# First stage of a two-layer attention kernel: the shared v products of two blocks in four 64x64 quarters, and a new order of the stage

## The chip, the cores and the metric

The kernel runs on one core of a Trainium2 chip. Its time is the device time of one execution in microseconds; the times of a kernel are given as the median of several runs. TensorE (PE) multiplies, VectorE (DVE), ScalarE (ACT) and GpSimd (POOL) do elementwise work, SyncE (SP) issues most DMA transfers.

## The reference

Two layers work on x of shape (4, 192, 128, 128), all in f32. Only the first part of the first layer matters here:

```python
qkv = dwconv3x3(conv1x1(x, w_qkv), w_dw)      # 192 -> 768 channels, then a 3x3 convolution of each channel alone
q, k, v, l = jnp.split(qkv, 4, axis=1)
...                                            # q, k normalised over the pixels, attention between channels
out = jnp.einsum('bhcd,bhdn->bhcn', attn, v)
pooled = jnp.mean(l, axis=(2, 3), keepdims=True)
...
```

The second layer is a dilated attention on the first one's output; its code isn't touched.

## The kernel before

The first stage (`project`, `plan_projection`) makes q, k and v by a 1x1 convolution, convolves v over 3x3, and writes q and k unconvolved to DRAM (the second stage convolves them). It works in 64 blocks: two images at a time, four image rows, 512 pixels of each image. The 192 input channels are 128 and 64. A block's `xt` tile (128 partitions, 3 x 512) holds the 128 first channels of both images in columns 0 and 1, and in column 2 the last 64 channels of the one image on partitions 0 to 63 and those of the other on 64 to 127 (`loads`, L347 to L351).

Each output tile of 128 channels is a sum of two products in one PSUM bank: a full one over 128 input channels (`first_half` L357, `first_half_v` L490) and one over the last 64 (`second_half` L362, `second_half_v` L495). The second ones use half of the array's rows, and those of the two images run side by side. There are three such tiles of q and k and one of v for each image. The 64 channels of v that are left make one tile of both images together, `shared_tile`: first (j = 0, L367) a full product with `wv2`, a 128x128 weight with the 64x64 weight twice on its diagonal and zeros elsewhere; then (j = 1, L371) two products of 128 rows by 64 columns, one for each image, side by side.

ScalarE moves the finished banks on: q and k to `us` (L375) and from there to DRAM (`qk_store`, L379), v to a ring of 12 rows (`v_evict`, L386), which is three blocks long. Three spare rows behind the ring's end are copied once per round (L175). The 3x3 convolution of a block's v (`plan_conv`) needs its neighbours' rows. For the 128-channel tiles ScalarE writes the centre tap to `pa` in PSUM (L397, one buffer), and VectorE adds eight taps (`tap`, L404), the last into `v_False`. For the shared tile ScalarE makes scaled copies (`side`, L416) and GpSimd adds them up (`side_sum`, L427). VectorE also adds up each block's x (`totals`, L441) for l's mean, and GpSimd keeps its edge columns (L445).

No loop sets the order. Every piece is given to a `Schedule` with an engine, a rank, a cost and what it comes after. The planner simulates the engines with these costs: an engine that is free takes the ready piece with the smallest rank, where on PE a piece of another array shape than the last counts `change_rank` more, and a change of shape takes `change` more time (0.13 and 0.05 in this stage before). The order found is emitted for each engine and is fixed from then on; the engines wait for one another by semaphores. `hold` makes the piece that takes a buffer come after the last user of the buffer that is taken again; the buffers of a pool are given out in the order of the first users' ranks. The products share six PSUM banks (`pu`), and `xt` has four buffers.

Of the kernel before, what the change touches and what calls it, by code (L numbers as in the profile page):

```python
# [13 lines left out]
B, C, H, W = 4, 192, 128, 128  # L14
# [9 lines left out]
PX = RB * W  # L24
RING = 12
# [11 lines left out]
class Schedule:  # L37
# [10 lines left out]
    def add(self, engine, rank, cost, run, after=(), shape=None, latency=LATENCY):  # L48
        op = dict(engine=engine, rank=rank, cost=cost, run=run, shape=shape, latency=latency, seq=len(self.ops))
        op.update(after=list(after), first=[], users=[], issued=[])  # L50
        self.ops.append(op)
        return op

    def hold(self, pool, bufs, first, last):

        self.pools.setdefault((pool, bufs), []).append((first, last))
# [131 lines left out]
    return t.rearrange("p (r w) -> p r w", w=W)  # L188


FULL, COLS, ROWS, QUADS = "128x128", "128x64", "64x128", "128x32"
HALVES = [slice(0, G), slice(G, 128)]
EXTRA = 2 * B * CH0 + B
SM = EXTRA + B * 2 * CH0
# [4 lines left out]
AROUND = (0, 1, 2, 6, 7, 8, 3, 5)  # L199

PLACES = {
# [111 lines left out]
def project(tc, x, load, other_loads, sums, qk_dram, v_dram, v2_dram):  # L316

    nc = tc.nc  # L320
    with ExitStack() as ctx:
        wts = ctx.enter_context(tc.tile_pool(name="p1w", bufs=1))
        wx, wx2, wv2, dwv = (load(wts, n) for n in ("wx", "wx2", "wv2", "dwv"))
        stage = Stage(ctx, tc, "p1", dict(xt=4, us=6, v=3, v2=3, side=3, ring=1), dict(pu=6, pa=1))
        rings = stage.pools["ring"]
        vboth = rings.tile([128, RING + SPARE, 2, W + 2], F32, tag="vboth", name="vboth")
        ring = [vboth[:, :, 0], vboth[:, :, 1]]
        ring.append(rings.tile([128, RING + SPARE, W + 2], F32, tag="ring2", name="ring2"))
        for r in ring:
            nc.gpsimd.memset(r[:, :, 0 : W + 2 : W + 1], 0.0)  # L330
        plan_projection(nc, stage, x, wx, wx2, wv2, dwv, vboth, ring, sums, qk_dram, v_dram, v2_dram)
        for i, run in enumerate(other_loads):
            stage.schedule.add("SP", 8 + i, 0.5, run)
        stage.run(tc)


def plan_projection(nc, stage, x, wx, wx2, wv2, dwv, vboth, ring, sums, qk_dram, v_dram, v2_dram):
    add, hold, tile_of, tiles = stage.schedule.add, stage.hold, stage.tile, stage.tiles
    mm = nc.tensor.matmul
    flat = lambda a: a.rearrange("c h w -> c (h w)")  # L340

    def place(n):
        p, i = divmod(n, NB)
        return 2 * p, slice(i * RB, (i + 1) * RB)

    def loads(n):
        im0, rows = place(n)  # L347
        t = tile_of("xt", ("xt", n), (128, 3, PX))
        nc.sync.dma_start(t[:, 0:2, :], x[im0 : im0 + 2, 0:128, rows, :].rearrange("b c h w -> c b (h w)"))
        for im in range(2):  # L350
            nc.sync.dma_start(t[HALVES[im], 2, :], flat(x[im0 + im, 128:C, rows, :]))  # L351

    def first_half(n, mt):

        for im in range(2):
            pu = tile_of("pu", ("pu", n, mt, im))
            mm(pu, wx[:, mt * 128 : (mt + 1) * 128], tiles["xt", n][:, im, :], start=True, stop=False)  # L357
# [3 lines left out]
            w = wx2[HALVES[im], mt * 128 : (mt + 1) * 128]  # L361
            mm(tiles["pu", n, mt, im], w, tiles["xt", n][HALVES[im], 2, :], start=False, stop=True)  # L362

    def shared_tile(n, j):

        if j == 0:
            mm(tile_of("pu", ("pu", n, 3, 2)), wv2, tiles["xt", n][:, 2, :], start=True, stop=False)  # L367
            return
        for im in range(2):
            to = tiles["pu", n, 3, 2][HALVES[im]]  # L370
            mm(to, wx[:, 2 * C + 128 :], tiles["xt", n][:, im, :], start=False, stop=True)  # L371
# [78 lines left out]
    def edge_row(n, to, of):  # L450
        nc.vector.tensor_reduce(sums[n // NB][2][:, :, to : to + 1], tiles["xt", n][:, :, of : of + W], AX.X, ALU.add)

    def plan_products(n):
        load_op = add("SP", n - 1.5, 0.5, (loads, n), latency=6.0)
        users = []
        shared = add("PE", n + 0.52, 0.86, (shared_tile, n, 0), [load_op], FULL)
        users.append(shared)
        for mt in range(4):
            t = n + 0.5 * (mt // 2) + 0.01 * (mt % 2)
            first, second = (first_half_v, second_half_v) if mt == 3 else (first_half, second_half)  # L460
            args = (n,) if mt == 3 else (n, mt)
            a = add("PE", t, 1.72, (first, *args), [load_op], FULL)
            b = add("PE", t + 0.2, 0.86, (second, *args), [a], ROWS)
            users += [a, b]
            if mt == 3:
                continue
            evs = [add("ACT", t + 0.25, 0.56, (qk_evict, n, mt, im), [b]) for im in range(2)]
            for ev in evs:
                hold("pu", a, ev)
            hold("us", evs[0], add("SP", t + 0.3, 0.3, (qk_store, n, mt), evs, latency=5.0))  # L470
            evs[1]["first"].append(evs[0])
        last = add("PE", n + 0.75, 0.9, (shared_tile, n, 1), [shared], COLS)
        users.append(last)
        for m in range(3):
            ev = add("ACT", n + 0.8, 0.56, (v_evict, n, m), [last if m == 2 else b])
            stage.fill("u", m, n, RING, ev)
            stage.repeat(ring, "u", m, n, RING, n + 0.83)
            hold("pu", shared if m == 2 else a, ev)
        users.append(add("DVE", n + 0.5, 1.7, (totals, n), [load_op]))
        users += [add("POOL", n + 0.3 * k, 0.2, (edges, n, k), [load_op]) for k in range(3)]  # L480
        if n % NB == 0:
            users.append(add("DVE", n, 0.5, (edge_row, n, 2, 0), [load_op]))
        if n % NB == NB - 1:
            users.append(add("DVE", n, 0.5, (edge_row, n, 0, PX - W), [load_op]))
        hold("xt", load_op, *users)

    def first_half_v(n):
# [7 lines left out]
            mm(tiles["pu", n, 3, im], w, tiles["xt", n][HALVES[im], 2, :], start=False, stop=True)  # L495

    def plan_conv(n):
        prev = first = add("ACT", n + 2, 1.2, (centre, n, False), latency=0.3)
        for j, t in enumerate(AROUND):
            prev = add("DVE", n + 2 + (j + 0.9) / 8, 1.22, (tap, n, t, j == 7), [prev])  # L500
            for m in range(2):
                stage.read("u", m, n, t // 3 - 1, prev)
        for m in range(2):
            stage.read("u", m, n, 0, first)
        hold("pa", first, prev)
        store = add("SP", n + 3.0, 0.3, (v_store, n, False), [prev], latency=5.0)
        hold("v", prev, store)
        prev = first = add("ACT", n + 2, 0.7, (centre, n, True))
        stage.read("u", 2, n, 0, first)
        for j, t in enumerate(AROUND):  # L510
            sd = add("ACT", n + 2 + (j + 0.4) / 8, 0.68, (side, n, t))
            stage.read("u", 2, n, t // 3 - 1, sd)
            prev = add("POOL", n + 2 + (j + 0.9) / 8, 1.26, (side_sum, n, t), [sd, prev])
            hold("side", sd, prev)
        store = add("SP", n + 3.0, 0.3, (v_store, n, True), [prev], latency=5.0)
        hold("v2", first, store)

    for n in range(2 * NB + 1):
        if n < 2 * NB:
            plan_products(n)  # L520
        if n >= 1:
            plan_conv(n - 1)
# [826 lines left out]
def _laid_out(inputs):  # L1349
    import numpy as np  # L1350

    a = {k: np.asarray(v) for k, v in inputs.items()}
# [12 lines left out]
    def both(w):  # L1365
        n = w.shape[1] // G
        z = np.zeros((2, G, n, 2, G), w.dtype)
        for im in range(2):
            z[im, :, :, im] = w.reshape(G, n, G)
        return z.reshape(128, n, 128)  # L1370
# [15 lines left out]
    for dy in range(3):  # L1386
# [5 lines left out]
    wx = wq[: 3 * C].T  # L1392
# [4 lines left out]
        "wx2": rest(wx),  # L1397
        "bands": bands,
        "cuttaps": cuttaps.reshape(4 * CH0, 2 * HEADS0, 3, 2 * CH0),
        "wv2": both(wx[128:, 2 * C + 128 :])[:, 0],  # L1400
        "wl": wq[3 * C :].T[:128],
        "wl2": rest(wq[3 * C :].T),
        "dwl": halves(dw[3 * C :]),
# [44 lines left out]
```

## Time and profile before

| | us |
|---|---|
| median of three runs (4406.96 to 4409.0) | 4407.45 |
| the profiled execution | 4406.01 |
| its span, first to last instruction | 4404.2 |
| first stage on PE | 8.27 to 852.7 |
| last tap of the first stage on DVE ends | 878.6 |

Over the whole span PE is busy 97%, DVE 86%, POOL 75%, ACT 59%. PE carries 80% of the chain that ended last; the first stage's groups on it are, with their busy time over the whole run:

| line | what | instructions | busy us |
|---|---|---|---|
| L357 | full products, q and k | 768 | 366.0 |
| L362 | products over the last 64 channels, q and k | 744 (to 830 us) | 193.3 |
| L490 | full products, v | 248 (to 830 us) | 119.3 |
| L371 | shared tile, 128x64 | 248 (to 830 us) | 66.9 |
| L495 | products over the last 64 channels, v | 248 (to 830 us) | 66.1 |
| L367 | shared tile, 128x128 with wv2 | 124 (to 830 us) | 63.3 |

A product of f32 shows as two instructions in the trace. A matmul's length in the trace is that of its way through the array; the distance of two starts is what it costs in a row. Times of one engine's groups overlap a little at their edges.

### The profile page before, as it was taken

The numbers are of one execution on the slowest core, as the hardware profiler recorded it, in microseconds if no ns is written. First come the engines' busy times: TensorE is split into PE (matmuls) and PEld (weight loads), VectorE is DVE, ScalarE is ACT, GpSimd is POOL, SyncE is SP. The second block draws the span as 40 slices with busy tenths as digits, with TensorE's granted clock in tenths as the row PEclk, the third lists the DMA queues.
The fourth block names the chain that finished last, engine by engine and source line by source line (L and its number), as shares of the span: only waits on it lengthen the run. The fifth ranks groups of instructions, "written<-read, shape, count | busy, mean of one in ns | idle before, by whom it ended". The sixth has DMA issues, their size and how long they took to land.

```text
span 4404.2 us, 64532 instructions
## 1 busy us (share of the span) xinstructions
PE 4289.9 (97%) x20608; PEld 1649.0 (37%) x20608; DVE 3806.3 (86%) x5492; ACT 2593.1 (59%) x4858; POOL 3319.0 (75%) x3407
## 2 busy tenths in 40 slices
PE   9999999899999998999999999999999999999996
PEld 3333333354445642333333333333333333333321
DVE  7998889855555546999999999999999999999996
ACT  7888888833333337656656556556566566566531
POOL 6777778811111112999999999999999999999998
PEclk9999999999999999999999999999999999999997
DMA  8777787668887648666566666656565665665521
GB/s 268 245 243 237 230 258 251 198 154 175 178 174 172 143 109 177 131 133 135 126 130 132 126 130 129 136 123 128 127 136 124 131 134 125 133 131 125 116 53 32
DMA packets 502386, 675.81 MB, mean 153 GB/s; under 512 B 138576, under 2 KB 320412, under 8 KB 502048
## 3 DMA queue, kind: packets, MB, share of 16 engines
q1 hardware_dynamic: 464160, 504.94, 43.2%
q0 software_dynamic: 37888, 166.74, 20.9%
q8 instruction: 166, 2.72, 0.3%
q14 instruction: 172, 1.41, 0.1%
HBM read 277.72 MB, written 201.33 MB: 109 GB/s over the span
## 4 chain that ended last, share of the span: by engine, by line
PE 80%; DVE 13%; issue 3%; POOL 2%; DMA 1%; ACT 1%; SPq 0%; DVEq 0%; POOLq 0%; ACTq 0%
PE pc L640 12%; PE sc L1105 9%; PE ex L1227 8%; PE pu L357 8%; PE ph L872 7%; PE pkv L1026 5%; DVE term L1233 4%; PE pu L362 4%; PE gram L712 4%; PE pkv L1029 4%; PE q L1086 4%; PE q L1083 4%; DVE prod L1094 3%; PE pu L490 2%; PE po L1249 2%
## 5 line engine op out<-in xcount | busy, mean ns | idle before, releaser
L1236 POOL TENSOR_TENSOR acc<-acc,term 128x512 f32<-128x512 f32 x1536 | 2034.6, 1330 | 133.0 <-DVE term L1233 45.5
L1233 DVE TENSOR_TENSOR term<-ex,vring 128x512 f32<-128x512 f32 (+2 forms) x1596 | 1000.1, 663 | 55.3 <-PE ex L1227 43.1
L1094 DVE TENSOR_TENSOR prod<-q,kring 128x1536 f32<-128x1536 f32 (+1 forms) x600 | 1007.3, 1688 | 16.8 <-PE q L1083 7.3
L427 POOL TENSOR_TENSOR v_True<-v_True,side 128x512 f32<-128x512 f32 (+1 forms) x512 | 647.9, 1267 | 169.7 <-ACT side L416 141.9
L404 DVE SCALAR_TENSOR_TENSOR pa<-vboth,dwv,pa 128x1024 f32<-128x1024 f32 (+1 forms) x448 | 574.3, 1282 | 76.9 <-ACT pa L397 54.4
L1227 PE MATMUL ex<-e_sb,spread 108*128 108x512 bf16 x1728 | 567.2, 387 | 37.5 <-DVE term L1233 31.2
L627 POOL COPY band<-band 64x384 f32<-64x384 f32 x192 | 95.8, 499 | 563.9 <-DMA band<-in_bands 506.5
L640 PE MATMUL pc<-u,band 64*64 64x508 f32 (+1 forms) x4608 | 518.3, 593 | 1.4 <-ACT ring L386 1.4
L1039 ACT COPY kring<-pkv 64x512 f32<-64x512 f32 x384 | 223.3, 581 | 419.5 <-PE pkv L1029 413.9
L924 DVE SCALAR_TENSOR_TENSOR pa<-hboth,posw,pa 128x1024 f32<-128x1024 f32 (+1 forms) x320 | 408.3, 1276 | 38.8 <-ACT pa L912 19.7
L1105 PE MATMUL sc<-prod,pick 128*32 128x512 f32 x3456 | 428.9, 598 | 1.8 <-DVE prod L1094 1.8
L653 DVE BATCH_NORM_STATS2 stats<-pc 128x6 f32<-128x128 f32 x1440 | 303.0, 283 | 141.1 <-ACT conv L649 141.0
L649 ACT COPY conv<-pc 128x512 f32<-128x512 f32 x384 | 210.6, 587 | 296.9 <-PE pc L640 288.7
L1026 PE MATMUL pkv<-y,wkv 128*128 128x512 f32 x768 | 365.5, 598 | 11.8 <-DMA y<-moved 8.7
L1227 PEld LDWEIGHTS <-spread 108*128 108x128 bf16 x1728 | 133.4, 98 | 647.0 <-issue 626.7
L872 PE MATMUL ph<-xv,mix 128*64 128x512 f32 (+1 forms) x1024 | 374.3, 596 | 0.5 <-DMA mix<-mixed 0.5
L357 PE MATMUL pu<-xt,wx 128*128 128x512 f32 x768 | 366.0, 613 | 8.3 <-DMA xt<-in_x 8.3
L1252 ACT COPY o<-po 128x512 f32<-128x512 f32 x192 | 106.2, 588 | 433.5 <-PE po L1249 227.9
L416 ACT ACTIVATE side<-ring,dwv 128x512 f32<-128x512 f32 (+1 forms) x512 | 350.8, 736 | 13.9 <-POOL v_True L427 13.1
L956 ACT ACTIVATE side<-hring,posw 128x512 f32<-128x512 f32 (+1 forms) x512 | 340.9, 710 | 9.6 <-DMA side<-side 7.7
L640 PEld LDWEIGHTS pc<-u,band 64*64 64x64 f32 x4608 | 189.5, 134 | 301.2 <-issue 284.7
L1039 ACT COPY vring<-pkv 64x512 f32<-64x512 f32 x384 | 223.9, 583 | 45.9 <-PE pkv L1029 32.6
(165 smaller groups left out, 6073.8 us busy)
## 6 DMA issues: line engine op xcount, KB each, us to landing
qk_dram<-us SPq DMA_DIRECT2D x192, 512.0 KB
u<-qk_dram SPq DMA_DIRECT2D x384, 256.0 KB
side<-side POOLq DMA_DIRECT2D x124, 768.0 KB, 7.1
xt<-in_x SPq DMA_DIRECT2D x64, 512.0 KB
v_dram<-v_False SPq DMA_DIRECT2D x64, 512.0 KB
xv<-in_x SPq DMA_DIRECT2D x128, 256.0 KB
xv<-v_dram SPq DMA_DIRECT2D x128, 256.0 KB
y<-moved POOLq DMA_DIRECT2D x64, 512.0 KB, 5.2
```

The costliest lines, as they stand in the source:

```text
L357: mm(pu, wx[:, mt * 128 : (mt + 1) * 128], tiles["xt", n][:, im, :], start=True, stop=False)
L404: nc.vector.scalar_tensor_tensor(by_row(to[:, o : o + length]), by_row(vboth[:, at : at + length, :, t % 3 : t % 3 + W]), dwv[:, 0, t : t ...
L427: nc.gpsimd.tensor_add(v[:, rows, :], v[:, rows, :], z[:, rows, :])
L640: nc.tensor.matmul(pcs[e][r * G : (r + 1) * G, :, to], band[at, e, c, dx, :], u[at, e, c, :].rearrange("p (b w) -> p b w", w=W)[:, :, of], ...
L872: mm(to, w[:, cols], tiles["xv", n, j, im], start=j == 0, stop=j == 2)
L1026: mm(rows3(tile_of("pc", key)), w, tiles["y", n, im], start=True, stop=False)
L1039: nc.scalar.copy(rows[HALVES[im], :, pad : pad + W], rows3(tiles["pkv", n, pair, im])[HALVES[e]])
L1094: nc.vector.tensor_mul(to[:, :, px].rearrange("p t (r w) -> p t r w", w=W), q.unsqueeze(1).to_broadcast([128, 3, *q.shape[1:]]), three,)
L1105: mm(sc[quad * 32 : (quad + 1) * 32, :], pick[:, QR - 4 * row : QR - 4 * row + 32], tiles["prod", n, k // NT, k % NT // 3][:, k % 3, :], s ...
L1227: mm(rows3(tile_of("ex", ("ex", n, g, t))), spread[:, t, :], e_sb, start=True, stop=True)
L1233: nc.vector.tensor_mul(rows3(to[:, px]), rows3(ex[:, px]), win)
L1236: nc.gpsimd.tensor_add(tiles["acc", n, g], tiles["acc", n, g], tiles.pop(("term", n, g, t)))
```

## The change

Three edits, all in the first stage.

The full product with `wv2` is gone, and so is `wv2`. For a pair of blocks n and n + 1, `shared_pair` makes the same sums by four products of 64 rows by 64 columns: for block n image 0 from array rows 0 to 63 to columns 0 to 63 and image 1 from rows 64 to 127 to columns 64 to 127; for block n + 1 the other two quarters. Since in these the rows and the columns are crossed, the images of the odd block must be exchanged: `loads` fetches the last 64 channels of odd blocks a second time, images swapped, to a new pool `xs` of two buffers. `shared_tile` keeps only its 128x64 products.

All ranks of the stage's pieces come from a table, `PLACES1`, by name and, for most, by the block's parity. The planner's costs for some pieces are changed, `change` is 0.2 and `change_rank` 3.9276.

```diff
+    "shared_pair": (-10.5337, 0),
+    "first_half0_0": (-11.0801, 0),
+    "first_half1_0": (-10.6217, 0),
+    "first_half2_0": (-10.7952, 0),
+    "first_half_v_0": (-10.8873, 0),
+    "first_half0_1": (-11.1547, 0),
+    "first_half1_1": (-11.0694, 0),
+    "first_half2_1": (-10.6251, 0),
+    "first_half_v_1": (-10.5823, 0),
+    "totals": (-11.7036, 0),
+    "centre0": (-10.4919, 0),
+    "tap": (-12.1176, 0),
...
-        stage = Stage(ctx, tc, "p1", dict(xt=4, us=6, v=3, v2=3, side=3, ring=1), dict(pu=6, pa=1))
+        stage = Stage(ctx, tc, "p1", dict(xt=4, xs=2, us=6, v=3, v2=3, side=3, ring=1), dict(pu=6, pa=1), change=(0.2, 3.9276))
...
+        if n % 2:
+            other = tile_of("xs", ("xs", n))
+            for im in range(2):
+                nc.sync.dma_start(other[HALVES[1 - im]], flat(x[im0 + im, 128:C, rows, :]))
...
-    def shared_tile(n, j):
-
-        if j == 0:
-            mm(tile_of("pu", ("pu", n, 3, 2)), wv2, tiles["xt", n][:, 2, :], start=True, stop=False)
-            return
+    def shared_pair(n):
+
+
+        for e in range(2):
+            to = tile_of("pu", ("pu", n + e, 3, 2))
+            of = tiles["xs", n + 1] if e else tiles["xt", n][:, 2, :]
+            for im in range(2):
+                half = HALVES[(im + e) % 2]
+                mm(to[HALVES[im]], wx2[half, 2 * C + 128 :], of[half], start=True, stop=False)
+
+    def shared_tile(n):
+
         for im in range(2):
             to = tiles["pu", n, 3, 2][HALVES[im]]
             mm(to, wx[:, 2 * C + 128 :], tiles["xt", n][:, im, :], start=False, stop=True)
...
+    def at(name, n, k=0):
+        first, step = PLACES1.get(name) or PLACES1[f"{name}_{n % 2}"]
+        return n + first + step * k
+
+    load_ops, pairs = {}, {}
+
     def plan_products(n):
-        load_op = add("SP", n - 1.5, 0.5, (loads, n), latency=6.0)
-        users = []
-        shared = add("PE", n + 0.52, 0.86, (shared_tile, n, 0), [load_op], FULL)
-        users.append(shared)
+        if n % 2 == 0:
+            for m in (n, n + 1):
+                load_ops[m] = add("SP", at("loads", m), 0.5, (loads, m), latency=6.0)
+            two = [load_ops[n], load_ops[n + 1]]
+            pairs[n] = pairs[n + 1] = add("PE", at("shared_pair", n), 0.86, (shared_pair, n), two, QUARTERS)
+        load_op, shared = load_ops[n], pairs[n]
+        users = [shared]
+        if n % 2:
+            hold("xs", load_op, shared)
...
-        last = add("PE", n + 0.75, 0.9, (shared_tile, n, 1), [shared], COLS)
+        last = add("PE", at("shared1", n), 0.86, (shared_tile, n), [shared], COLS)
...
-            prev = add("DVE", n + 2 + (j + 0.9) / 8, 1.22, (tap, n, t, j == 7), [prev])
+            prev = add("DVE", at("tap", n, j), 1.24, (tap, n, t, j == 7), [prev])
```

More of the change, by code (lines that the diff above doesn't have):

```diff
@@ L188, in rows3 @@
     return t.rearrange("p (r w) -> p r w", w=W)
-FULL, COLS, ROWS, QUADS = "128x128", "128x64", "64x128", "128x32"
+FULL, COLS, ROWS, QUADS, QUARTERS = "128x128", "128x64", "64x128", "128x32", "64x64"
 HALVES = [slice(0, G), slice(G, 128)]
@@ L199 @@
 AROUND = (0, 1, 2, 6, 7, 8, 3, 5)
+PLACES1 = {
+    "loads": (-10.5941, 0),
+    "shared_pair": (-10.5337, 0),
+    "first_half0_0": (-11.0801, 0),
+    "second_half0_0": (-9.1745, 0),
+    "qkev0_0": (-12.2520, 0),
+    "qkst0_0": (-12.2622, 0),
+    "first_half1_0": (-10.6217, 0),
+    "second_half1_0": (-11.4242, 0),
+    "qkev1_0": (-12.1789, 0),
+    "qkst1_0": (-5.5430, 0),
+    "first_half2_0": (-10.7952, 0),
+    "second_half2_0": (-8.3455, 0),
+    "qkev2_0": (-12.1932, 0),
+    "qkst2_0": (-19.1101, 0),
+    "first_half_v_0": (-10.8873, 0),
+    "second_half_v_0": (-6.7221, 0),
+    "shared1_0": (-11.0929, 0),
+    "vev0_0": (-9.4687, 0),
+    "vev1_0": (-11.4742, 0),
+    "vev2_0": (-11.4466, 0),
+    "totals": (-11.7036, 0),
+    "edges": (-10.7962, 0.00202),
+    "edge_row": (-16.1943, 0),
+    "first_half0_1": (-11.1547, 0),
+    "second_half0_1": (-12.4945, 0),
+    "qkev0_1": (-11.6485, 0),
+    "qkst0_1": (-2.8082, 0),
+    "first_half1_1": (-11.0694, 0),
+    "second_half1_1": (-10.5482, 0),
+    "qkev1_1": (-11.5669, 0),
+    "qkst1_1": (-12.2544, 0),
+    "first_half2_1": (-10.6251, 0),
+    "second_half2_1": (-8.7956, 0),
+    "qkev2_1": (-11.3820, 0),
+    "qkst2_1": (-12.1897, 0),
+    "first_half_v_1": (-10.5823, 0),
+    "second_half_v_1": (-10.5833, 0),
+    "shared1_1": (-7.9665, 0),
+    "vev0_1": (-12.0997, 0),
+    "vev1_1": (-16.1908, 0),
+    "vev2_1": (-11.6989, 0),
+    "centre0": (-10.4919, 0),
+    "tap": (-12.1176, 0),
+    "vst0": (-11.5571, 0),
+    "centre1": (-9.3757, 0),
+    "side": (-10.4725, 0.19535),
+    "side_sum": (-11.0068, 0.00009),
+    "vst1": (-12.1054, 0),
+}
 PLACES = {
@@ L322, in project @@
         wts = ctx.enter_context(tc.tile_pool(name="p1w", bufs=1))
-        wx, wx2, wv2, dwv = (load(wts, n) for n in ("wx", "wx2", "wv2", "dwv"))
-        stage = Stage(ctx, tc, "p1", dict(xt=4, us=6, v=3, v2=3, side=3, ring=1), dict(pu=6, pa=1))
+        wx, wx2, dwv = (load(wts, n) for n in ("wx", "wx2", "dwv"))
+        stage = Stage(ctx, tc, "p1", dict(xt=4, xs=2, us=6, v=3, v2=3, side=3, ring=1), dict(pu=6, pa=1), change=(0.2, 3.9276))
         rings = stage.pools["ring"]
@@ L330, in project @@
             nc.gpsimd.memset(r[:, :, 0 : W + 2 : W + 1], 0.0)
-        plan_projection(nc, stage, x, wx, wx2, wv2, dwv, vboth, ring, sums, qk_dram, v_dram, v2_dram)
+        plan_projection(nc, stage, x, wx, wx2, dwv, vboth, ring, sums, qk_dram, v_dram, v2_dram)
         for i, run in enumerate(other_loads):
@@ L334, in project, with plan_projection @@
         stage.run(tc)
-def plan_projection(nc, stage, x, wx, wx2, wv2, dwv, vboth, ring, sums, qk_dram, v_dram, v2_dram):
+def plan_projection(nc, stage, x, wx, wx2, dwv, vboth, ring, sums, qk_dram, v_dram, v2_dram):
     add, hold, tile_of, tiles = stage.schedule.add, stage.hold, stage.tile, stage.tiles
@@ L451, in edge_row @@
         nc.vector.tensor_reduce(sums[n // NB][2][:, :, to : to + 1], tiles["xt", n][:, :, of : of + W], AX.X, ALU.add)
+    def at(name, n, k=0):
+        first, step = PLACES1.get(name) or PLACES1[f"{name}_{n % 2}"]
+        return n + first + step * k
+    load_ops, pairs = {}, {}
     def plan_products(n):
-        load_op = add("SP", n - 1.5, 0.5, (loads, n), latency=6.0)
-        users = []
-        shared = add("PE", n + 0.52, 0.86, (shared_tile, n, 0), [load_op], FULL)
-        users.append(shared)
+        if n % 2 == 0:
[7 more added lines that the diff above has]
+            hold("xs", load_op, shared)
         for mt in range(4):
-            t = n + 0.5 * (mt // 2) + 0.01 * (mt % 2)
+            kind = "_v" if mt == 3 else mt
             first, second = (first_half_v, second_half_v) if mt == 3 else (first_half, second_half)
             args = (n,) if mt == 3 else (n, mt)
-            a = add("PE", t, 1.72, (first, *args), [load_op], FULL)
-            b = add("PE", t + 0.2, 0.86, (second, *args), [a], ROWS)
+            a = add("PE", at(f"first_half{kind}", n), 1.72, (first, *args), [load_op], FULL)
+            b = add("PE", at(f"second_half{kind}", n), 0.86, (second, *args), [a], ROWS)
             users += [a, b]
@@ L466, in plan_products @@
                 continue
-            evs = [add("ACT", t + 0.25, 0.56, (qk_evict, n, mt, im), [b]) for im in range(2)]
+            evs = [add("ACT", at(f"qkev{mt}", n, im), 0.54, (qk_evict, n, mt, im), [b]) for im in range(2)]
             for ev in evs:
                 hold("pu", a, ev)
-            hold("us", evs[0], add("SP", t + 0.3, 0.3, (qk_store, n, mt), evs, latency=5.0))
+            hold("us", evs[0], add("SP", at(f"qkst{mt}", n), 0.3, (qk_store, n, mt), evs, latency=5.0))
             evs[1]["first"].append(evs[0])
-        last = add("PE", n + 0.75, 0.9, (shared_tile, n, 1), [shared], COLS)
+        last = add("PE", at("shared1", n), 0.86, (shared_tile, n), [shared], COLS)
         users.append(last)
         for m in range(3):
-            ev = add("ACT", n + 0.8, 0.56, (v_evict, n, m), [last if m == 2 else b])
+            ev = add("ACT", at(f"vev{m}", n), 0.54, (v_evict, n, m), [last if m == 2 else b])
             stage.fill("u", m, n, RING, ev)
-            stage.repeat(ring, "u", m, n, RING, n + 0.83)
+            stage.repeat(ring, "u", m, n, RING)
             hold("pu", shared if m == 2 else a, ev)
-        users.append(add("DVE", n + 0.5, 1.7, (totals, n), [load_op]))
-        users += [add("POOL", n + 0.3 * k, 0.2, (edges, n, k), [load_op]) for k in range(3)]
+        users.append(add("DVE", at("totals", n), 1.65, (totals, n), [load_op]))
+        users += [add("POOL", at("edges", n, k), 0.2, (edges, n, k), [load_op]) for k in range(3)]
         if n % NB == 0:
-            users.append(add("DVE", n, 0.5, (edge_row, n, 2, 0), [load_op]))
+            users.append(add("DVE", at("edge_row", n), 0.5, (edge_row, n, 2, 0), [load_op]))
         if n % NB == NB - 1:
-            users.append(add("DVE", n, 0.5, (edge_row, n, 0, PX - W), [load_op]))
+            users.append(add("DVE", at("edge_row", n), 0.5, (edge_row, n, 0, PX - W), [load_op]))
         hold("xt", load_op, *users)
@@ L497, in plan_conv @@
     def plan_conv(n):
-        prev = first = add("ACT", n + 2, 1.2, (centre, n, False), latency=0.3)
+        prev = first = add("ACT", at("centre0", n), 1.1, (centre, n, False), latency=0.3)
         for j, t in enumerate(AROUND):
-            prev = add("DVE", n + 2 + (j + 0.9) / 8, 1.22, (tap, n, t, j == 7), [prev])
+            prev = add("DVE", at("tap", n, j), 1.24, (tap, n, t, j == 7), [prev])
             for m in range(2):
@@ L505, in plan_conv @@
         hold("pa", first, prev)
-        store = add("SP", n + 3.0, 0.3, (v_store, n, False), [prev], latency=5.0)
+        store = add("SP", at("vst0", n), 0.3, (v_store, n, False), [prev], latency=5.0)
         hold("v", prev, store)
-        prev = first = add("ACT", n + 2, 0.7, (centre, n, True))
+        prev = first = add("ACT", at("centre1", n), 0.66, (centre, n, True))
         stage.read("u", 2, n, 0, first)
         for j, t in enumerate(AROUND):
-            sd = add("ACT", n + 2 + (j + 0.4) / 8, 0.68, (side, n, t))
+            sd = add("ACT", at("side", n, j), 0.64, (side, n, t))
             stage.read("u", 2, n, t // 3 - 1, sd)
-            prev = add("POOL", n + 2 + (j + 0.9) / 8, 1.26, (side_sum, n, t), [sd, prev])
+            prev = add("POOL", at("side_sum", n, j), 1.28, (side_sum, n, t), [sd, prev])
             hold("side", sd, prev)
-        store = add("SP", n + 3.0, 0.3, (v_store, n, True), [prev], latency=5.0)
+        store = add("SP", at("vst1", n), 0.3, (v_store, n, True), [prev], latency=5.0)
         hold("v2", first, store)
@@ L1399, in _laid_out @@
         "cuttaps": cuttaps.reshape(4 * CH0, 2 * HEADS0, 3, 2 * CH0),
-        "wv2": both(wx[128:, 2 * C + 128 :])[:, 0],
         "wl": wq[3 * C :].T[:128],
```

## The prediction

> **What bounds the kernel now.** I read the busy slices first, then the first stage by windows, then its timeline, and last the place where the next stage takes over. The change touches the first stage only.
>
> ```profile
> PE   9999999899999998999999999999999999999996
> ...
> DVE  7998889855555546999999999999999999999996
> ```
>
> A slice is 110 us. TensorE is full through the first seven; VectorE is close behind. The first stage in windows gives the spare time of each engine (columns: stretch, length, then busy us and instructions of PE, weight loads, DVE, ACT, POOL, then clock, DMA share, GB/s):
>
> ```profile
> 100.00:850.00 750.00, 748.93 (x2168) 271.31 (x2166) 679.24 (x534) 658.50 (x1138) 596.17 (x615) 1.00 0.74 240
> ```
>
> PE idles 1 us of 750 at full clock. These are 57 blocks of 13.16 us, so DVE is busy 11.92 us a block, ACT 11.55, POOL 10.46. Now one block in the timeline, first PE (start, length, engine, line), then DVE:
>
> ```profile
> 508.89 3.70 PE L357 MATMUL pu<-xt,wx 128*128 128x512 f32 x8
> 512.52 1.99 PE L362 MATMUL pu<-xt,wx 64*128 64x512 f32 x8
> 514.44 1.99 PE L357 MATMUL pu<-xt,wx 128*128 128x512 f32 x4
> 516.35 1.13 PE L362 MATMUL pu<-xt,wx 64*128 64x512 f32 x4
> 517.41 1.99 PE L490 MATMUL pu<-xt,wx 128*128 128x512 f32 x4
> 519.23 1.02 PE L367 MATMUL pu<-xt,wv 128*128 128x512 f32 x2
> 520.19 1.13 PE L495 MATMUL pu<-xt,wx 64*128 64x512 f32 x4
> 521.24 1.08 PE L371 MATMUL pu<-xt,wx 128*64 128x512 f32 x4
> ```
>
> ```profile
> 510.29 1.75 DVE L441 TENSOR_REDUCE xsum<-xt 128x3 f32<-128x1536 f32 x1
> 511.95 9.23 DVE L404 SCALAR_TENSOR_TENSOR pa<-vboth,dwv,pa 128x1024 f32<-128x1024 f32 x7
> 521.21 1.28 DVE L404 SCALAR_TENSOR_TENSOR v_False<-vboth,dwv,pa 128x1024 f32<-128x1024 f32 x1
> 522.41 1.75 DVE L441 TENSOR_REDUCE xsum<-xt 128x3 f32<-128x1536 f32 x1
> ```
>
> Each matmul appears as two instructions, so x8 on L357 is four matmuls. On L362 x8 is four too, but they take 1.92 us (512.52 to 514.44), because two 64-row matmuls run at once. A block is 14 matmul-times: 8 full and 1 shared full (L367), 4 for the paired 64-row ones, 1 for the paired 64-column ones (L371). Seven shape changes lie in this block, which lasts 13.36 us, to the next L357 group at 522.25. Other blocks have five and take 12.96 (L357 at 36.36, then 49.32). Two changes are therefore 0.40 us, **0.20 us a change**, and (12.96 - 1.0)/14 = **0.854 us a matmul-time**. The PE timeline of the whole stage has 369 changes, 5.77 a block. 64 x 14 x 0.854 + 369 x 0.20 = 839 us, plus two PE waits of 1.03 and 1.07 and a first group of 5.86 instead of 3.63, is 843; PE's first stage runs 8.27 to 852.7, 844.4. So the sum accounts for it: 13.19 us a block, PE and its shape changes, nothing else.
>
> The end of the stage is not PE's:
>
> ```profile
> 857.02 9.24 DVE L404 SCALAR_TENSOR_TENSOR pa<-vboth,dwv,pa 128x1024 f32<-128x1024 f32 x7 [4.33 <-ACT pa L397]
> ...
> 877.34 1.28 DVE L404 SCALAR_TENSOR_TENSOR v_False<-vboth,dwv,pa 128x1024 f32<-128x1024 f32 x1
> 878.77 0.47 PE L553 MATMUL pl<-reach,wl 128*96 128x9 f32 x2 [16.40 <-DVE v_False L404]
> ```
>
> The convolutions of the last two blocks follow the last eviction, and PE waits 16.4 us for DVE before the next stage runs on. What counts is when DVE's last tap ends: about 61 block periods, between a start and a tail of two convolutions that the change leaves alone.
>
> **The change, part by part.**
>
> Shared product. One full matmul-time per block (L367) becomes one set of four quarter matmuls per two blocks. If the four run at once, that is 14 to 13.5 matmul-times: 0.427 us a block. Here a rule speaks against the edit. In this set two quarters with different rows write the two halves of one PSUM bank. The row that shows it is the next stage's convolution, which orders its 64x64 quarters over two banks in the same crossed way:
>
> ```profile
> L640 PE MATMUL pc<-u,band 64*64 64x508 f32 (+1 forms) x4608 | 518.3, 593 | 1.4 <-ACT ring L386 1.4
> ```
>
> 518.3/4608 is 0.112 us an instruction, 0.225 a matmul: a quarter of 0.854 with some loss, so four at once. The Trainium skill, "TensorEngine Tiling (Array Packing)", section "Gotcha 1: PSUM Pressure", says that different row tiles cannot access the same PSUM bank at the same time. By that rule the four, in their order (bank 0, 0, 1, 1), would need three steps, 2.56 us a pair or 1.28 a block, and this part would lose 0.43 us a block (61 x 0.43 = 26 us). By the row it gains 0.43 (26 us). Here the row decides: the same shapes, type and bank pattern.
>
> Shape changes. The new order needs a count. PSUM has six banks for these products; each product pair, and each shared pair, takes two, so three are in flight. By the new ranks their order in two blocks is qk0, v, qk2, qk1, shared, then qk0, qk1, qk2, v of the odd block. A change is now charged 3.93 ranks, nearly four blocks, so PE leaves a shape only when nothing of it is ready. Following that by hand, full products come in groups of two or three pairs (limited by the banks), each followed by its 64-row halves: three such rounds in two blocks, 6 changes, plus one into quarters and one into columns (both blocks' column matmuls together). 8 in two blocks, 4 a block. Bounds: 3 if rounds merge, 5.8 if they break up as they do now. PE then needs 13.5 x 0.854 + 4 x 0.20 = **12.33 us a block** (12.13 to 12.69).
>
> Larger groups press on ACT: after a group of three, the next group needs the first pair's banks. Its two evictions (0.49 apart, 0.6 the last, from the rows of L375) are done some 1.5 us after its 64-row half, while the other two halves hide 1.9. That is a small margin; if an ACT side product (0.72) is in the way each time, it costs up to 0.3 a round, 0.45 a block. I take about 0.1.
>
> DVE. It executes what it did before. Its floor from the lines above: 511.95 to 521.21 is 9.26 for seven taps, 1.20 to the totals at 522.41, and 1.66 for these (510.29 to 511.95): **12.12 us a block**. It holds only if the totals fill the gap in which ACT writes the next centre into the single pa buffer (1.12 us). ACT has 0.28 us to spare there: with an empty gap the next tap starts 2.58 us after the last one's start (866.29 to 868.87) against 2.86 with the totals inside. At 12.33 DVE has 0.2 us a block left where it has 1.07 now, so late centres begin to show. Between 0 and 0.79 (the 41.6 us of DVE waiting for centres in the 53 blocks from 50 to 750, all harmless today); I take 0.1 beyond PE's need, since those waits are largely DVE being early.
>
> Other parts. ACT's 11.55 and POOL's 10.46 fit. The exchanged x adds 2 x 128 KB per two blocks to some 3.16 MB a block (240 GB/s x 13.16): the DMA share goes from 0.74 to 0.74 x 1.04 x 13.19/12.45 = 0.82, and it has been 0.93 at 289 GB/s from 50 to 100 us without starving PE. SP gets one more issue a block on average (some 0.6 us) beside nine. The x tiles have four buffers and the shared pair wants both blocks' loads, but it stands fifth among nine, so both are there; if a load were late, PE behind it would stand. wv2's load, issued ahead of the first x (0.47 us), goes: 0 to 0.5, taken as 0.
>
> Sum: 12.33 + 0.1 + about 0.02 = **12.45 us a block**, and 61 x (13.19 - 12.45) = **45 us**. The profiled execution took 4406.01 (span 4404.2), so its like would take 4361; the median shown is 1.4 higher, hence 4362.
>
> **Rivals**, as periods P, time 4407.4 - 61 x (13.19 - P).
>
> 1. PE no longer bounds and DVE does, with late centres: P = 12.12 + 0.5 to 0.79 = 12.65 to 12.9, 4374 to 4390. For it: 0.2 us of slack, and planned tap costs of 1.24 where taps start 1.32 apart, so the order is planned for a faster DVE. Against: today's waits are those of an engine with time to spare. Chance 0.22.
> 2. Fuller groups: three changes a block and no late centre, P = 12.12 to 12.3, 4342 to 4353. For: PE waits almost nowhere now. Against: three engines would be at 95% or more in strict order. Chance 0.14.
> 3. Slower: the totals fall between taps instead of into the centre's gap. Then a block is 9.26 + 2.58 + 1.66 = 13.50 on DVE, 4426. A share s of blocks gives 12.12 + 1.38 s; it reaches 13.33, slower by 0.2%, at s = 0.88. Against: taps are ranked ahead of the totals of later blocks, which leaves the gaps for these. Chance 0.05.
> 4. The quarters take turns at a bank: P = 12.45 + 0.85 = 13.3, about 4414, or the gain is eaten by waits for banks: no measurable change, 4400 to 4414. Chance 0.03.
>
> My forecast, P = 12.3 to 12.65 (4353 to 4374), has 0.56. Two runs of this kernel differ by less than 0.2%, some 9 us, and only more than that counts as a change. The range drops about half of rival 2 and the far end of rival 1, with 3 and 4: 4346 to 4387. Faster 0.92, same 0.03, slower 0.05.
>
> **What would show it.** Quarters: x8 instructions in about 1 us, where 2 us or more means turns at a bank. Shape changes: near 256 in the stage. PE from 8 to about 805, DVE's last tap near 833, and PE's wait for it still some 16 us. PE waits for ACT's evictions above 0.5 us a block, or DVE waits for pa as large and PE no longer full, point to rival 1. I am wrong if DVE's first-to-last tap spacing does not fall, or if a later stage changes its length.

## The result, and the profile after

The changed kernel takes **4361.93 us** (median of four runs, 4361.5 to 4362.7) where the kernel before takes 4407.74: a ratio of 0.9896, 95% interval 0.9884 to 0.9909. Measured again on two chips, the ratio was 0.9899 (0.9884 to 0.9914) and 0.9902 (0.9887 to 0.9916). The forecast was 4362.

The agreement is better than the steps behind it. Here are two profiles of the kernel before and three of the changed one, cut at the start of the first stage's last tap on DVE ("the rest" below is what comes after this cut):

| us | PE's first stage ends | last tap starts | span | from there to the end |
|---|---|---|---|---|
| before | 852.8 | 877.3 | 4404.2 | 3526.9 |
| before, second profile | 852.8 | 877.4 | 4406.0 | 3528.6 |
| changed | 814.8 | 838.7 | 4359.7 | 3521.0 |
| changed, second | 813.3 | 837.2 | 4363.7 | 3526.5 |
| changed, third | 814.3 | 838.2 | 4362.8 | 3524.6 |

The first stage became 38.7 to 40.2 us shorter, where 45 were forecast. The rest, whose code is the same, came out 5.9 us shorter in the first pair of profiles.

In the stage itself, the windows first (columns as before):

```profile
100.00:800.00 700.00, 697.26 (x2256) 264.51 (x2256) 674.49 (x532) 659.28 (x1128) 588.97 (x615) 1.00 0.85 266
```

PE is still full (697 of 700 us), and DVE has gone from 91% to 96%, ACT from 88% to 94%. Next, two blocks in PE's timeline:

```profile
502.32 1.99 PE L418 MATMUL pu<-xt,wx 64*128 64x512 f32 x8
504.24 0.65 PE L428 MATMUL pu<-xt,wx 64*64 64x512 f32 x2
504.25 0.65 PE L428 MATMUL pu<-xs,wx 64*64 64x512 f32 x2
504.71 0.60 PE L428 MATMUL pu<-xt,wx 64*64 64x512 f32 x2
504.73 0.60 PE L428 MATMUL pu<-xs,wx 64*64 64x512 f32 x2
505.25 1.94 PE L434 MATMUL pu<-xt,wx 128*64 128x512 f32 x8
507.12 5.42 PE L413 MATMUL pu<-xt,wx 128*128 128x512 f32 x12
512.47 2.85 PE L418 MATMUL pu<-xt,wx 64*128 64x512 f32 x12
515.25 1.98 PE L564 MATMUL pu<-xt,wx 128*128 128x512 f32 x4
...
520.59 1.13 PE L569 MATMUL pu<-xt,wx 64*128 64x512 f32 x4
...
523.37 3.70 PE L413 MATMUL pu<-xt,wx 128*128 128x512 f32 x8
527.00 1.99 PE L418 MATMUL pu<-xt,wx 64*128 64x512 f32 x8
```

The order is the one worked out by hand: full products in groups of three, three and two pairs, each followed by its 64-row halves, then the quarters and both blocks' column products. The four quarters run their two passes together, from 504.24 and from 504.71, and the next shape starts 1.01 us after the first: one matmul-time and a change. From 502.32 to 527.00 are 24.68 us, **12.34 a block** against 12.33 forecast, and the stage has 257 shape changes.

DVE's lines are where they were, only closer:

```profile
606.40 9.24 DVE L467 SCALAR_TENSOR_TENSOR pa<-vboth,dwv,pa 128x1024 f32<-128x1024 f32 x7
615.68 1.28 DVE L467 SCALAR_TENSOR_TENSOR v_False<-vboth,dwv,pa 128x1024 f32<-128x1024 f32 x1
616.88 1.75 DVE L504 TENSOR_REDUCE xsum<-xt 128x3 f32<-128x1536 f32 x1
618.54 9.30 DVE L467 SCALAR_TENSOR_TENSOR pa<-vboth,dwv,pa 128x1024 f32<-128x1024 f32 x7
```

606.40 to 618.54 is 12.14: DVE at its floor of 12.12, with the totals in the centre's gap. The next stage still waits for DVE's last tap, but for 7.91 us (8.7 and 9.1 in the other two profiles) and not for some 16 as forecast (timeline at the end of the stage):

```profile
838.67 1.28 DVE L467 SCALAR_TENSOR_TENSOR v_False<-vboth,dwv,pa 128x1024 f32<-128x1024 f32 x1
...
840.10 0.46 PE L627 MATMUL pl<-reach,wl 128*96 128x9 f32 x2 [7.91 <-DVE v_False L467]
```

Before this wait PE runs 72 product instructions of the second stage. They took 8.1 us in the kernel before (from 854.25) and take 15.2 here (from 816.95), with a short wait for a DMA (0.92) and a granted clock of 0.50 for part of the time. As DVE ends later still, this costs nothing.

At 12.34 a block, PE's stage would be 790 us long. It is 806.8. The rest of it stands in a few places, most of them early. The timeline of all engines from 38 us:

```profile
39.79 0.33 POOL L508 COPY xcol<-xt 128x8 f32<-128x8 f32 x2 [6.65 <-DMA xt<-in_x]
...
41.57 0.20 POOL L508 COPY xcol<-xt 128x8 f32<-128x8 f32 x1 [1.45 <-DMA xt<-in_x]
41.72 7.63 POOL L490 TENSOR_TENSOR v_True<-v_True,side 128x512 f32<-128x512 f32 x6
...
43.02 0.72 ACT L479 ACTIVATE side<-ring,dwv 128x512 f32<-128x512 f32 x1 [7.52 <-POOL v_True L490]
43.65 1.06 ACT L449 COPY vboth<-pu 128x512 f32<-128x512 f32 x2
44.27 6.08 PE L413 MATMUL pu<-xt,wx 128*128 128x512 f32 x7 [3.82 <-ACT vboth L449]
```

Read from the top: GpSimd's edge columns wait for x of a block; its side sums stand behind them in its queue; ScalarE's side product waits for a buffer that these sums free; the v evictions stand behind that product; PE waits 3.82 us for a bank. Two more such chains follow. At 73.8 PE waits 2.01, after GpSimd has done five copies for the second stage's bands (65.7 to 70.0) in between. At 399 it waits 2.58, after DVE has done 3.6 us of work on the first image pair's gate (381.3 to 384.9). The granted clock can fall as well. The window from 44 to 46 us:

```profile
44.00:46.00 2.00, 1.73 (x2) 0.84 (x3) 1.26 (x1) 2.00 (x5) 1.92 (x3) 0.50 1.09 297
```

It is 0.50 there, and the group after the wait takes 6.43 us where it takes 3.63 later on; the group at 73.8 takes 5.31. Waits of 8.6 us, 2.8 and 1.7 for these two groups, and 2.2 in the very first one (which the kernel before has too) make 15.3 of the 16.8.

### The profile page after: what moved, and what is told of

Same layout as the page of the kernel before. It is cut to its first block, busy times and chain, and to the rows that moved or that the text cites. A ratio compares the mean times of both kernels' runs of the same rounds, so it can differ in the third digit from the quotient of the medians.

```text
span 4359.7 us, 64790 instructions
## 1 busy us (share of the span) xinstructions
PE 4248.5 (97%) x20736; PEld 1639.7 (38%) x20736; DVE 3805.5 (87%) x5492; ACT 2602.5 (60%) x4858; POOL 3316.0 (76%) x3407
## 4 chain that ended last, share of the span: by engine, by line
PE 78%; DVE 14%; issue 4%; POOL 2%; DMA 1%; ACT 1%; SPq 0%; DVEq 0%; POOLq 0%; ACTq 0%
PE pc L714 12%; PE sc L1179 9%; PE ex L1301 8%; PE ph L946 7%; PE pu L413 7%; PE pkv L1100 5%; DVE term L1307 4%; PE gram L786 4%; PE pkv L1103 4%; PE q L1160 4%; PE q L1157 4%; PE pu L418 3%; DVE prod L1168 3%; PE pu L564 2%; PE po L1323 2%
```

## The experiments

All are edits of the changed kernel, but for old_order and before_again, which start from the kernel before. Times are medians; "stage" is the start of DVE's last tap in the profile (changed kernel: 837.2 to 838.7).

| run | us | ratio to the kernel before (95%) | stage |
|---|---|---|---|
| full_pair | 4383.65 | 0.9947 (0.9932 to 0.9962) | 855.0 |
| old_order | 4389.22 | 0.9956 (0.9941 to 0.9971) | 860.2 |
| loads_late | 4359.70 | 0.9891 (0.9874 to 0.9907) | 832.4 |
| totals_third | 4362.79 | 0.9899 (0.9884 to 0.9914) | 834.8 |
| totals_more | 4398.12 | 0.9976 (0.9967 to 0.9984) | 869.5 |
| no_stick | 4489.35 | 1.0185 (1.0168 to 1.0202) | 962.4 |
| uncrossed | 4381.69 | 0.9940 (0.9925 to 0.9955) | 853.5 |
| after_again | 4363.29 | 0.9899 (0.9884 to 0.9914) | 837.2 |
| split | 4381.64 | 0.9947 (0.9931 to 0.9964) | 853.9 |
| after_5 | 4362.21 | 0.9902 (0.9887 to 0.9916) | 838.2 |
| loads_late_5 | 4358.29 | 0.9893 (0.9878 to 0.9908) | 833.0 |
| before_again | 4407.52 | 1.0000 (0.9992 to 1.0009) | 877.4 |

### What the quarters are worth

**full_pair** keeps the order and takes the quarters back:

```diff
-            of = tiles["xs", n + 1] if e else tiles["xt", n][:, 2, :]
-            for im in range(2):
-                half = HALVES[(im + e) % 2]
-                mm(to[HALVES[im]], wx2[half, 2 * C + 128 :], of[half], start=True, stop=False)
+            mm(to, wv2, tiles["xt", n + e][:, 2, :], start=True, stop=False)
```

> The changed kernel with the same order of PE's work, but each shared pair made by two full products with the old diagonal weight, and no second load of x. PE then has 14 matmul-times a block instead of 13.5 and still 4 shape changes. If PE bounds the stage (the prediction): 64 x 0.427 = 27 us more than the changed kernel, about 4389 us. If DVE or ACT bound it by now, a good part of this is hidden: under 15 us more, below 4377. If the quarters only paid through the order that they allow: no difference.

It took 21.7 us more, its stage 16 to 18. PE's own time rose by what was forecast: its stage is 822.9 us with 1.7 of waits, against 806.8 with 8.6 of waits and 4.5 of slow clock, so 821.2 to 793.7, **27.5**. But this kernel, with 0.43 us more slack a block and no second load, has none of the waits at the start. So of the 27 us, some 10 were given back to waits, and to the slow clock behind them, that the tighter stage has.

**uncrossed** keeps quarters, but the same two for both blocks:

```diff
-            of = tiles["xs", n + 1] if e else tiles["xt", n][:, 2, :]
+            of = tiles["xt", n + e][:, 2, :]
             for im in range(2):
-                half = HALVES[(im + e) % 2]
+                half = HALVES[im]
```

> The changed kernel, with the shared product of odd blocks in the same two quarters as that of even blocks, so without the second load with the images exchanged. If only different quarters run at once, a pair takes two matmul-times, 1.71 us instead of 0.85: PE as in the kernel with full products, about 4384. If the array takes all four in one time anyway, or the load is a burden: 4362 or less.

4381.7, as full_pair. Its quarter groups take 1.86 us to the next shape where the changed kernel's take 1.01, so two that share a quarter follow one another:

```profile
508.79 1.93 PE L424 MATMUL pu<-xt,wx 64*64 64x512 f32 x8
```

The second load of x is what buys the half matmul-time.

**old_order** is the other half of the change undone: the kernel before, with its ranks, costs and change of shape, and only `loads`, `shared_pair` and `shared_tile` of the changed one (shared pair at rank n + 0.52).

> The kernel before with its own ranks, costs and change of shape, and only the shared product put into quarters with the exchanged load. Its planned order has some 5.3 shape changes a block. If a block costs PE its matmul-times and 0.20 us a change: 13.5 x 0.854 + 5.3 x 0.20 = 12.59 us, 61 x (13.19 - 12.59) = 37 us below the kernel before, 4371. If the new order is what brings the gain and quarters alone give little, it stays within 10 us of the kernel before, 4398 or more.

Missed: 4389.2, 18.5 us below the kernel before, in between the two theories. The count was right (340 changes in the stage, 5.3 a block), so PE's own time is 806 us. But its stage is 833.8: PE waits 18.4 us for evictions, 7.2 of them at 44.6 us and others through the whole stage (0.75 at 508, 1.96 at 662). Of the other 9 us, 2.2 are the slow first group again; the granted clock is 0.50 from 39.8 to 50.1 and from 818.1 to 821.5 us, which accounts for most of what is left. The old order, fed with half a matmul-time less, ran into its evictions. The new order (ranks, costs and change of shape together) brings the larger half of the gain: without it quarters give 18.5 us of 45, and with it full products already give 24. That 24 has its sum too: 112 changes fewer (257 instead of 369) at 0.20 are 22 us.

### What a change of shape costs

**no_stick**: `change=(0.2, 3.9276)` to `change=(0.2, 0.05)`, all ranks as in the changed kernel.

> The changed kernel with its ranks, but with the old weight of 0.05 ranks on a change of shape: the planned order has 6.5 changes a block instead of 4. If a change costs PE 0.20 us: 13.5 x 0.854 + 6.5 x 0.20 = 12.83 us a block, 0.5 more than the changed kernel, less the 10 us or so of waits at the start that more slack hides: 4380 to 4390. If changes are hidden by the matmuls around them: about as the changed kernel, 4362, or less where the ranks alone give the gain.

Missed by 100 us: 4489, slower than the kernel before. The windows show where (150 to 780 us):

```profile
150.00:780.00 630.00, 583.57 (x1742) 194.98 (x1740) 522.14 (x405) 516.49 (x877) 455.12 (x482) 0.99 0.74 231
```

Every engine idles, PE 46 us of 630 and DVE 108. The ranks and the weight on a change of shape are one set: with the ranks alone the planner makes an order in which the engines wait for one another in turn. So this run says nothing of a change's price, and **split** was made for that. In the emitted order it takes one 64-row half of each group of three ahead of the third full pair:

```diff
+def apart(ops):
+    pe = [o for o in ops if o["engine"] == "PE"]
+    for i in range(len(pe) - 5):
+        six = pe[i : i + 6]
+        if i and pe[i - 1]["shape"] == FULL or [o["shape"] for o in six] != [FULL] * 3 + [ROWS] * 3:
+            continue
+        at = next(r for r in six[3:] if six[2] not in r["after"])
+        ops = [o for o in ops if o is not at]
+        ops.insert(next(k for k, o in enumerate(ops) if o is six[2]), at)
+    return ops
...
-            for op in self.schedule.order():
+            for op in apart(self.schedule.order()):
```

> The changed kernel with one thing moved: in each group of three full pairs followed by their three 64-row halves, one of the halves goes ahead of the third full pair. No matmul, load or eviction is added, and banks come free earlier, if anything; only the shape changes go from 8 to 12 in two blocks. If a change costs PE 0.20 us: the period of two blocks goes from 24.69 to 25.49 us, 61 x 0.4 = 24 us, of which the slack at the start hides some 8 to 12: 4374 to 4386. If the large loss of the order planned with the old weight was the changes themselves (over 1 us each): far above, 4450 or more. If changes cost nothing: 4362 and a period of 24.7.

4381.6. From one set of quarters to the next on PE:

```profile
330.91 0.65 PE L440 MATMUL pu<-xt,wx 64*64 64x512 f32 x2
...
356.39 0.65 PE L440 MATMUL pu<-xt,wx 64*64 64x512 f32 x2
```

25.48 us against 24.68: four changes more are 0.80, **0.20 us each**, with the same products. This confirms the price that the forecast had taken from periods of 12.96 and 13.36.

### Whether DVE bounds

**totals_third** takes two thirds of the totals away from DVE:

```diff
-        nc.vector.tensor_reduce(sums[p][0][:, :, i : i + 1], tiles["xt", n], AX.X, ALU.add)
+        nc.vector.tensor_reduce(sums[p][0][:, 0:1, i : i + 1], tiles["xt", n][:, 0:1, :], AX.X, ALU.add)
```

> The changed kernel, with the totals of x for a third of the columns only (the l mean leaves out two thirds of x): some 1.1 us a block less on DVE. If PE bounds (the prediction): at most 3 us less, 4359 or more. If late centres or DVE's own floor bound the stage: up to the 16 us by which PE's stage exceeds 64 blocks of 12.34, 4346 to 4354.

4362.8: nothing. (Its stage is 2.4 to 3.9 us shorter: it has one spell of half clock where the changed kernel's profiles have two, of which one is twice as long.) The freed time became waiting, as the waits of 100 to 780 us show (total, times, longest), first of the changed kernel, then of this one:

```profile
DVE pa L467 <- ACT pa L460: 2.1, 8, 0.3
```

```profile
DVE pa L468 <- ACT pa L461: 52.2, 52, 1.7
```

PE bounds the stage. In the changed kernel late centres cost DVE next to nothing.

**totals_more** adds that third a second time instead.

> The changed kernel, with the first third of each block's totals taken a second time on DVE: 0.6 us a block more (0.68 long, overlapping a little). DVE's floor goes from 12.12 to 12.7 us a block, past PE's 12.34. If DVE really stands only 0.2 us behind PE (the prediction): 61 x 0.37 = 23 us more than the changed kernel, 4384. If DVE has more room than its floor says, for example through centres that come early: under 10 us more.

34.8 us more than the changed kernel on the same chip, where 23 were expected. DVE's lines say why:

```profile
560.84 1.75 DVE L504 TENSOR_REDUCE xsum<-xt 128x3 f32<-128x1536 f32 x1
562.62 0.69 DVE L505 TENSOR_REDUCE xsum<-xt 128x1 f32<-128x512 f32 x1
563.22 9.30 DVE L467 SCALAR_TENSOR_TENSOR pa<-vboth,dwv,pa 128x1024 f32<-128x1024 f32 x7
...
576.14 9.23 DVE L467 SCALAR_TENSOR_TENSOR pa<-vboth,dwv,pa 128x1024 f32<-128x1024 f32 x7
```

The two reductions don't overlap, so the addition is 0.72 (1.78 + 0.60 to the next tap, instead of 1.66), and a block takes 12.92 or (from 576.14 to the next such line at 588.98) 12.84, the average 12.88: DVE without a gap. 61 x (12.88 - 12.34) = 33 us; the stage rose by 32.4. So DVE does stand some 0.2 us a block behind PE: what a next change saved on PE beyond that would be lost by these figures.

### The waits at the start, and the rest of the kernel

**loads_late** makes each later-stage load come after the x load of a block (`plan_projection` returns `load_ops` for it):

```diff
-            stage.schedule.add("SP", 8 + i, 0.5, run)
+            stage.schedule.add("SP", 8 + i, 0.5, run, [load_ops[8 + i]])
```

> The changed kernel, with the weights of later stages loaded one by one behind the x of blocks 8 and on, instead of all between 15 and 30 us. If the wait of 3.8 us of PE at 40 us comes from x tiles that are late behind these loads (GpSimd's edge columns wait for x, its sums stand behind them, ScalarE's side products behind these, the evictions behind those), the wait and the slow clock after it go: 3.8 + 2.8 = 6.6 us, about 4355. If the wait has another cause, for example the rings filling for the first time, nothing changes.

The stage ended 5 to 6 us earlier, PE's stage is 800.1 us instead of 806.8, and the waits at 44 and 74 us and the slow clock behind them are gone (one of 1.65 at 35 us is new, behind the second stage's band copies on GpSimd). From 40 to 100 us, this kernel and the changed one:

```profile
40.00:100.00 60.00, 60.00 (x202) 22.48 (x202) 54.37 (x42) 53.96 (x94) 47.72 (x50) 1.00 0.92 284
```

```profile
40.00:100.00 60.00, 54.17 (x164) 20.41 (x160) 49.13 (x37) 46.85 (x80) 46.99 (x65) 0.91 0.90 282
```

But its time was only about 2 us lower, where 6.6 were expected. **after_again**, the changed kernel unedited, was run to see whether that is scatter.

> The changed kernel once more. The first stage should end its taps at 838 to 840 us again; what is open is how far the rest of the kernel, 3521 us after the last tap's start here and 3525 to 3529 in other kernels with the same later code, differs from execution to execution. If the 3521 belongs to the changed kernel it comes back within 1 us; if it is scatter, the rest is nearer 3525.

Its rest took 3526.5 us, so the 3521.0 didn't come back. **after_5** and **loads_late_5** are the two kernels again on one chip.

> The changed kernel beside the one with later loads, on one chip: 4362 to 4363 us; the last tap starts at 837 to 839 us, the rest of the kernel takes 3524 to 3527.

> The kernel with the later stages' weights loaded behind block 8 once more, now beside the changed kernel: its first stage ended its last tap 5 to 6 us earlier (832.4 us), its time was only 2 us lower. If the rest of the kernel is scatter: 4 to 6 us below the changed kernel in the medians, and the last tap at 832 to 833 again. If the later loads take something from the second stage: again 2 us or less.

4362.2 and 4358.3, with rests of 3524.6 and 3524.8. The stage's 5 us (838.2 to 833.0) is shown in both pairs of profiles; in the times the ranges still overlap (4359.4 to 4365.5 and 4356.4 to 4361.4), so loads_late is likely, not surely, the fastest of these kernels, by some 4 us. Last, **before_again**.

> The kernel before once more, for a second profile of it: its last tap starts at 877 to 878 us again (the stage is settled by PE), the rest took 3526.9 us in its first profile. If the rest is scatter in both kernels: anywhere from 3521 to 3529. If the changed kernel's later stages are really shorter (3521.0, 3526.5 and 3524.6 so far): 3527 or more.

The stage came back to 0.1 us, the rest was 3528.6. In the changed kernel the rests lie between 3521.0 and 3526.5, in the eight runs of its edits between 3523.3 and 3527.3, in the kernel before at 3526.9 and 3528.6, in old_order at 3528.8.

A good part of this difference can be seen just behind the stage. From the last tap's start to the second stage's first matmul into `gram` it is 75.1 and 75.4 us in the kernel before and 72.5 to 72.8 in the changed one. PE's instructions between them are the same, but one group, which starts some 36 us after the last tap, has a granted clock of 0.50 for its first 3.4 us before and of 1.00 after:

```profile
913.83 7.00 PE L640 MATMUL pc<-u,band 64*64 64x512 f32 x46
```

```profile
873.92 5.35 PE L714 MATMUL pc<-u,band 64*64 64x512 f32 x46
```

Another, of 24 instructions, takes 5.37 and 4.14 us. totals_more has the later code of the changed kernel, and yet it has the slow groups (7.04 and 5.37) and 75.6 us. So these 2.6 us or so come from the clock in an execution, and not from other code. But scatter need not be all: in three measurements the medians of the two kernels lie 43.4 to 45.8 us apart, and the stages profiled there only 38.7 to 40.2. So 4 to 7 us come back each time. Whether the later stages gain them or the profiled executions had a longer stage than most stays open.

## Why the prediction was right

The range held; what bounds the stage, and why the change makes it shorter, came out as forecast. That the forecast was met to 0.1 us is luck: two of its terms were off and cancelled.

- **PE bounds, 0.854 us a matmul-time and 0.20 a change**: shown. Split measures 0.20, full_pair and uncrossed 27.5 and 26.7 us for half a matmul-time a block (822.1 less 1.7 of waits for uncrossed, to 793.7) where 27.3 follow from 64 x 0.427.
- **Four quarters at once, two of them in one bank**: shown, 1.01 us a set with its change. The rule of the Trainium skill, "TensorEngine Tiling (Array Packing)", "Gotcha 1: PSUM Pressure", that was weighed there doesn't hold for these quarters, which write different halves of a bank's partitions. Uncrossed shows that what excludes two at once is the same quarter.
- **4 changes a block, 12.33 us**: 257 changes and 12.34.
- **The waits**: the 0.1 us a block that the sum set aside for late centres and evictions isn't there in the steady state, where PE hardly waits. In its place stand three waits and the slow clock behind them, 13 us in all, at the start and at the image boundary. The sum took start and tail as unchanged; the start is not (DVE's first tap even comes 4 to 5 us earlier, at 21.9 to 22.1 us, before these waits). About half of these 13 us come from the other stages' loads, as loads_late shows (806.8 to 800.1). The sum said PE's end near 805 and the last tap near 833; they were 813 to 815 and 837 to 839. Since the sum had kept 0.1 a block (6 us), the stage fell short by 5 to 6 only.
- **The rest unchanged**: it was 5.9 us shorter in the first pair of profiles and some 4 in the means, and that made up for the stage. The forecast had named a later stage of another length as a sign of being wrong, and over all pairs of profiles the rest is 0.4 to 7.6 us shorter. Some 2.6 us of this are the clock behind the last tap; the cause of the other part is not shown. PE's wait for the last tap, said to stay at 16 us, became 8 to 9.
- **Rivals**: DVE as the bound is refuted by totals_third, and totals_more shows how near it is. DVE's first and last tap lie 815.1 to 816.8 us apart, in the kernel before 850.8 and 851.3. The totals stayed in the centre's gap. Quarters did not take turns. Groups fuller than three pairs did not come.

## What to carry to other kernels

Count a stage in the bound engine's own units (matmul-times and shape changes here) and check the count against two kinds of period in the trace; then a new order can be priced by hand before it runs. The price holds only while the bound engine hardly waits: for old_order and no_stick the same count was 18 and 100 us too low. Check how far the second engine stands behind, since that distance is the most that the next saving can bring. When slack gets thin, look for work in the stage that belongs to others, such as later stages' loads and copies: here PE's waits were 2.1 us in the kernel before and became 8.6.

## What the runs showed of the hardware

A short wait of PE can halve its granted clock, or not, and this differs between executions of one kernel. The three waits in the three profiles of the changed kernel, with what the clock did at each:

| PE waits | first profile | second | third |
|---|---|---|---|
| 3.7 to 4.1 us, at 44 us | 0.50 for 6.8 us | 0.50 for 6.8 us | 0.50 for 6.8 us |
| 2.0 us, at 73 us | 0.50 for 3.4 us | stays 1.00 | stays 1.00 |
| 2.6 us, at 398 us | stays 1.00 | 0.50 for 3.4 us | 0.50 for 3.4 us |

In the kernel before, after waits of 1.0 to 1.5 us, it stayed at 1.00. The Trainium skill, "TensorE: Matmul & The Clock Gate", Part 1, tells of a free-running window of 3.4 us, so that its phase differs from run to run. The differing outcomes, and spells of 3.4 us or twice that, fit this; but where the page has the clock fall after an idle window of some 3.4 us, here waits of 2.0 to 2.6 us were enough. It is one source of the scatter that I had not reckoned with, in the stage (6.8 and 3.4 us at half clock lose some 5 us of full speed) and behind it (the slow groups after the last tap).
